# Cross-attention on one core: another order of the opening loads and query chunks, and a closing sum in two halves

## The chip, the cores and the metric

The kernel runs on one core of a Trainium2 chip. The metric is device microseconds from launch to end, the median of several runs. One execution was also taken by the hardware profiler; its trace times every instruction on the tensor engine (PE, with its weight loads shown as PEld), the vector engine (DVE), the scalar engine (ACT), GpSimd (POOL) and the sync engine (SP), and every DMA. DMAs are issued here by SP and by ACT, each through a queue of its own (q1 is SP's in the trace, q10 is ACT's).

## The reference, cut to what matters

Two token sets of 2048 rows attend with 20 heads of 32 channels to 77 text tokens and, separately, to 77 image tokens. The two attentions are added, projected by Wo, and bias and input are added.

```python
q = _split_heads(hidden_states @ Wq.T, H)                 # (2, 20, 2048, 32)
k, v = heads(text @ Wk.T), heads(text @ Wv.T)             # 77 text tokens
k_ip, v_ip = heads(ip @ Wk_ip.T), heads(ip @ Wv_ip.T)     # 77 image tokens
out = merge(attend(q, k, v)) + merge(attend(q, k_ip, v_ip))
return out @ Wo.T + bo + residual
```

## The kernel before, in words

All operands are float32 and lie with the contracted dimension first. The 640 channels are five chunks of 128 (`NC`), so one chunk holds four heads; the tokens of a batch are four blocks of 512 (`TB`). A step `u` is one channel chunk over half of a batch's tokens, that is two blocks `h` = 0, 1; there are 20 steps. Chunk number `q` is `u // 2`.

For a block and a chunk, `queries` (L193 to L205) makes five matmuls of 128x512, one for each slice of 128 input channels (`k`), into one of eight PSUM banks, and `take_queries` (L207) lets ACT copy the bank, scaled, to a tile `qT`. `project_kv` (L136) makes eight matmuls of 128x154 for the keys or values of one chunk, from the context (`wo_ct`) and a weight (in slots of `aT`). `scores` (L220) makes a group of scores: for each of up to three token tiles four matmuls, one into each bank of a half (banks 0 to 3 or 4 to 7). A group then goes through ACT, DVE and POOL for the softmax; `attend` multiplies by the values; the last stage multiplies by Wo in a scheme of sums and products (`F` words) and adds each product into its sums on DVE (`Y` words, `add_part`, L784), and a finished sum is stored by a DMA.

The order on every engine is written by hand: the opening is plain code (L522 to L558), and everything behind it is a table of words, `SCHEDULE`, that `emit` turns into instructions one after the other. `R0.0@0` is score group 0 of step 0 in banks 0 to 3, `q.1.0@0` the query chunk of step 1, block 0 in bank 0, `cq.1.0` ACT's copy of it, `K0.0` ACT's copies of the scores, `v.0.0@1` a value projection, `LK`, `LQ`, `LX` loads. Each engine runs its instructions in that order, and a semaphore wait holds up all that stands behind it on the same engine. Each hardware DMA takes the next of eight completion counters, in turn over both queues, and waits until the DMA that used that counter before has landed; so no more than eight are under way.

The opening, before: x's block 0 (`x_82` below) comes in five slices of 256 KB and the first chunk of Wq in five of 64 KB, alternating between SP and ACT (L524 to L526); then SP alone loads block 1 (`x_83`), the second chunk of Wq, the context and the two key weights in turn, then blocks 2 and 3 and the value weights. PE makes seven matmuls on zeros (L547), then three query chunks one after the other (step 0 on blocks 0 and 1, step 2 on block 0; L549 to L551), then the two key projections (L552 to L555), and the table begins with the score groups `R0.0`, `R1.0`.

## Time and profile before

| | us |
|---|---|
| three runs | 498.40, 498.75, 499.44 (median 498.75) |
| the profiled execution | 497.84 |
| its span, first to last instruction | 496.0 |
| PE busy | 489.1 (99% of the span) |
| DVE busy | 413.0 (83%) |
| POOL busy | 370.3 (75%) |
| ACT busy | 301.4 (61%) |

The profiled execution took 497.84 us, 1.84 us more than its span and 0.91 us less than the median of the runs. In the trace one float32 matmul is two records, so a query chunk is ten. A row of the timeline gives start, length, engine, line, operation, result and operands, the number of records, and in brackets how long the engine had been idle and what ended that.

### The profile page before, as it was taken

To read this page: it belongs to the slowest core of one execution; us is meant where nothing else is said; L and a number is where in the kernel's file an instruction comes from. 1 tells how busy PE (TensorE), PEld (TensorE's weight loads), DVE (VectorE), ACT (ScalarE), POOL (GpSimd) and SP (SyncE) were. 2 spreads that over 40 slices of the span, in tenths; PEclk is the share of its full clock that TensorE was granted. 3 is DMA by queue.
4 is the path that set the end of the run, shared out by engine and by line. 5 is a ranking of instruction groups with operands and counts; after the bars stand their busy time and mean duration, and the time that the engine had idled before them with its cause. 6 is when DMAs were issued, how large, how long until landed. Compare 5 with 4: busy or idle time off the path is not lost.

```text
span 496.0 us, 10378 instructions
## 1 busy us (share of the span) xinstructions
PE 489.1 (99%) x4114; PEld 288.5 (58%) x4114; DVE 413.0 (83%) x417; ACT 301.4 (61%) x929; POOL 370.3 (75%) x158
## 2 busy tenths in 40 slices
PE   8999999999999999999999999999999999999997
PEld 4676657467467556456556654754755675444442
DVE  0069999979999989979979796777999888999885
ACT  1175858977687778677999869677666962100000
POOL 0069998889988989788977798365989989249820
PEclk9999999999999999999999999999999999999999
DMA  8994404142425435395671359344551221510125
GB/s 267 351 260 128 120 3 130 49 112 74 109 65 170 125 120 165 119 380 204 194 236 49 113 159 316 133 127 140 166 174 45 62 91 42 171 63 23 43 85 211
DMA packets 67472, 69.38 MB, mean 140 GB/s; under 512 B 5472, under 2 KB 47200, under 8 KB 67424
## 3 DMA queue, kind: packets, MB, share of 16 engines
q1 hardware_dynamic: 66704, 68.00, 43.6%
q8 instruction: 32, 0.52, 0.5%
q10 hardware_dynamic: 720, 0.72, 0.5%
q14 instruction: 16, 0.13, 0.1%
HBM read 54.94 MB, written 10.49 MB: 132 GB/s over the span
## 4 chain that ended last, share of the span: by engine, by line
PE 95%; DMA 3%; SPq 1%; ACTq 0%; ACT 0%; DVE 0%; issue 0%
PE bank L199 33%; PE bank L846 11%; PE bank L330 11%; PE bank L231 11%; PE bank L488 10%; PE bank L140 9%; PE bank L469 7%; PE bank L498 3%; DMA aT<-in_L_xattn_Wk_ip_dram 2%; DMA x<-in_x_dram 1%; SPq L532 1%; ACTq L526 0%; SPq L130 0%; DVE acc L792 0%; ACT pb L243 0%
## 5 line engine op out<-in xcount | busy, mean ns | idle before, releaser
L314 POOL TENSOR_TENSOR pb<-pb,rden 128x1848 f32<-128x1848 f32 (+1 forms) x60 | 175.9, 2943 | 25.6 <-DVE rden L309 25.0
L199 PE MATMUL bank<-x,wq 128*128 128x512 f32 x400 | 179.6, 598 | 1.5 <-DMA x<-in_x_dram 1.4
L293 POOL TENSOR_TENSOR pb<-pb,mx 128x1848 f32<-128x1848 f32 (+1 forms) x42 | 128.2, 3066 | 58.5 <-DVE mx L279 58.3
L199 PEld LDWEIGHTS bank<-x,wq 128*128 128x128 f32 x400 | 73.5, 190 | 87.4 <-issue 81.6
L321 DVE STREAM_TRANSPOSE pb<-pb 128x1920 f32<-128x1920 f32 (+1 forms) x60 | 115.5, 1935 | 6.7 <-POOL pb L314 6.7
L279 DVE TENSOR_REDUCE mx<-pb 128x24 f32<-128x1848 f32 (+1 forms) x51 | 93.8, 1850 | 32.0 <-ACT pb L243 31.8
L243 ACT COPY pb<-bank 128x462 f32<-128x462 f32 (+1 forms) x204 | 87.1, 537 | 34.6 <-PE bank L231 34.0
L304 DVE TENSOR_REDUCE den<-pb 128x24 f32<-128x1848 f32 (+1 forms) x49 | 91.5, 1875 | 18.6 <-ACT pb L299 15.8
L299 ACT ACTIVATE pb<-pb 128x1848 f32<-128x1848 f32 (+1 forms) x42 | 69.3, 1651 | 18.6 <-POOL pb L293 18.5
L231 PEld LDWEIGHTS bank<-kT,qT 32*128 32x128 f32 x1280 | 45.5, 184 | 26.3 <-issue 16.6
L267 ACT ACTIVATE pb<-bank,mx 128x77 f32<-128x77 f32 x184 | 53.1, 380 | 10.8 <-DVE mx L282 10.8
L231 PE MATMUL bank<-kT,qT 32*128 32x154 f32 x1280 | 56.6, 306 | 0.3 <-ACT kT L557 0.3
L330 PE MATMUL bank<-pb,v 32*32 32x512 f32 x1600 | 55.2, 597 | 0.0
L267 ACT ACTIVATE pb<-pb,mx 128x77 f32<-128x77 f32 x160 | 47.3, 373 | 0.0
L140 PE MATMUL bank<-wo_ct,aT 128*128 128x154 f32 x320 | 45.8, 297 | 0.4 <-DMA aT<-in_L_xattn_Wk_ip_dram 0.4
L140 PEld LDWEIGHTS bank<-wo_ct,aT 128*128 128x128 f32 x320 | 42.8, 188 | 3.4 <-issue 2.2
L330 PEld LDWEIGHTS bank<-pb,v 32*32 32x32 f32 x1600 | 30.6, 103 | 21.6 <-issue 9.2
L209 ACT ACTIVATE qT<-bank 128x512 f32<-128x512 f32 x40 | 24.2, 614 | 27.4 <-PE bank L199 27.4
L267 ACT ACTIVATION_READ_ACCUMULATOR pb<-bank,mx 128x1 f32 x144 | 36.7, 258 | 0.0
L469 PE MATMUL bank<-aT,wo_ct 128*128 128x512 f32 x80 | 36.4, 595 | 0.0
L488 PE MATMUL bank<-aT,wo_ct 128*128 128x256 f32 x128 | 32.0, 384 | 0.0
L488 PEld LDWEIGHTS bank<-aT,wo_ct 128*128 128x128 f32 x128 | 23.8, 190 | 7.7 <-issue 4.5
(76 smaller groups left out, 427.9 us busy)
## 6 DMA issues: line engine op xcount, KB each, us to landing
x<-in_x_dram SPq DMA_DIRECT2D x20, 1280.0 KB, 7.3
out_dram<-acc SPq DMA_DIRECT2D x20, 256.0 KB, 2.6
x<-in_x_dram SPq DMA_DIRECT2D x18, 256.0 KB, 5.4
acc<-in_x_dram SPq DMA_DIRECT2D x16, 256.0 KB, 3.4
out_dram<-x SPq DMA_DIRECT2D x15, 256.0 KB, 2.0
v<-vS SPq DMA_DIRECT2D x160, 20.0 KB, 2.1
wq<-in_L_xattn_Wq_dram SPq DMA_DIRECT2D x9, 320.0 KB, 4.7
aT<-in_L_xattn_Wk_dram SPq DMA_DIRECT2D x5, 512.0 KB, 5.5
```

The costliest lines, as they stand in the source:

```text
L140: nc.tensor.matmul(keys_in(out), loaded[n][:, k, :], cT[:, k, :, t, :], start=(k == 0), stop=(k == NCC - 1))
L199: nc.tensor.matmul(pq, wqs[q % 3][:, k, :], xs[place_of(u, h)][:, k, :], start=(k == 0), stop=(k == NC - 1),)
L231: nc.tensor.matmul(ps[g][:, ts(t, 2 * L)], qTs[(u, h)][g * D : (g + 1) * D, ts(st, P)], kT[g * D : (g + 1) * D, c, b].rearrange("p t l -> ...
L243: nc.scalar.copy(keys_of(u, s)[:, :, g], ps[g][:, : n * 2 * L].rearrange("p (n l) -> p n l", n=n))
L267: nc.scalar.activation(row, row if ps is None else rows_in(ps[g], n)[:, t, x], AF.Exp, bias=maxs[(u, s)][:, *one], accum_out=None if den i ...
L279: nc.vector.tensor_reduce(mx, rows_of(u, s), AX.X, ALU.max, negate=negate)
L293: nc.gpsimd.tensor_tensor(rows_of(u, s), rows_of(u, s), maxs[(u, s)].unsqueeze(3).to_broadcast([P, n, 2, L]), ALU.subtract)
L304: nc.vector.tensor_reduce(den_of(u, s), rows_of(u, s), AX.X, ALU.add)
L314: nc.gpsimd.tensor_tensor(rows_of(u, s), rows_of(u, s), rdens[(u, s)].unsqueeze(3).to_broadcast([P, n, 2, L]), ALU.mult)
L321: nc.vector.transpose(p, p)
L330: nc.tensor.matmul(pa[r][g * D : (g + 1) * D, :], v4s[q % 2][rows, g, k, :], zones[rows, :, g, k, :], start=(k == 0), stop=(k == NK - 1),)
L488: nc.tensor.matmul(part, w_of[m][:, kp, op], t_of(m, b, i)[:, kp], start=(op == kp == 0 and m in (1, 2, 5)), stop=(op == 1 and kp == 1 and ...
```

## The change

In the opening the first block of x is multiplied slice by slice: for each slice of x's block 0, one matmul of step 0 and one of step 2, into two banks side by side, and the first slice in two halves of 256 tokens. The key projections follow, then the score group `R0.0`, and only then the query chunk of step 0 on block 1 (`q.0.1@4 cq.0.1`, new words in the table behind `R0.0@0`). The first three chunks of Wq lie in slots of `aT` that are free until later (`wq_first`): chunks 0 and 1 come together in rows of 1 KB, chunk 2 by itself. The context is loaded by SP and the two key weights by ACT; x's block 1, Wq's chunk 2, block 2, the value weights and block 3 follow on SP. Five matmuls on zeros stand in place of seven. Eight early `qT` tiles go to free slots of `aT` instead of the pool of five. At the end, the last product (`F32.0`) and the last sum (`Y4.0.20`) are made in two halves of 256 columns, the first half stored by SP, the second by ACT. All other words of the table stay in their order.

```diff
+    EARLY = {(2, 0): 8, (2, 1): 9, (3, 0): 10, (3, 1): 11, (4, 0): 16, (4, 1): 17, (5, 0): 18, (5, 1): 19}
+    SIDES = slice(0, HT), slice(HT, TB)
+    wq_first = aT[:, ds((NC - 2) * NHB, NHB), :].rearrange("p s t -> p (s t)")[:, : NC * 3 * P]
...
-    for k in range(NC):
-        load_x(queues[k % 2])
-        queues[1 - k % 2].dma_start(out=wqs[0][:, k, :], in_=WqT[ts(k, P), :P])
-    for _ in range(NC):
-        load_x()
-    load_wq(1)
+    for n, cols in enumerate(SIDES):
+        queues[n].dma_start(out=xs[0][:, 0, cols], in_=xT[:P, cols])
+        load_first(nc.scalar, 0, n, n + 1)
+    for k in range(1, NC):
+        load_x(queues[k % 2])
+        load_first(queues[1 - k % 2], k, 0, 2)
+    for k in (0, half):
+        load_ctx(k)
+        load_w(k // half, nc.scalar)
+    for _ in range(NC):
+        load_x()
+    nc.sync.dma_start(out=wq_first[:, :, 2], in_=WqT[:, ts(2, P)].rearrange("(k p) o -> p k o", p=P))
...
-    for _ in range(7):
+    for _ in range(5):
         nc.tensor.matmul(banks[0][:, :P], warm, warm, start=True, stop=True)
-    FIRST = ((0, 0), (0, 1), (2, 0))
-    for n, (u, h) in enumerate(FIRST):
-        queries(u, h, banks[G + n])
-        take_queries(u, h, banks[G + n])
+    first = [(2 * c, 0, banks[G + c]) for c in range(2)]
+    for n, cols in enumerate(SIDES):
+        for c, (_, _, pq) in enumerate(first):
+            nc.tensor.matmul(
+                pq[:, cols], wq_first[:, 0, c], xs[0][:, 0, cols], start=(n == 0), stop=False, skip_group_check=True
+            )
+    for k in range(1, NC):
+        for u, h, pq in first:
+            queries(u, h, pq, (k,), loose=True)
+    for u, h, pq in first:
+        take_queries(u, h, pq)
...
-        "R0.0@0 R1.0@1 K0.0 q.1.0@0
+        "R0.0@0 q.0.1@4 cq.0.1 R1.0@1 K0.0 q.1.0@0
...
+            for cols in sides:
+                nc.vector.tensor_tensor(t[:, cols], t[:, cols], ps[:, cols], op)
...
+            for queue, cols in zip(queues, sides):
+                queue.dma_start(out=outT[ts(m, P), tokens], in_=t[:, cols])
```

First place: PE in the opening, from the matmuls on zeros to the first score group. `bank_71` to `bank_74` are banks 4 to 7, `x_82` and `x_83` are x's blocks 0 and 1, and L140 (L143 after the change) is a key projection. Before:

```order
L547 MATMUL bank_67<-pb 128x128 x7
L199 MATMUL bank_71<-x_82,wq_75 128x512 x5
L199 MATMUL bank_72<-x_83,wq_75 128x512 x5
L199 MATMUL bank_73<-x_82,wq_76 128x512 x5
L140 MATMUL bank_69<-wo_ct,aT 128x154 x8
L140 MATMUL bank_74<-wo_ct,aT 128x154 x8
L231 MATMUL bank_67<-kT,qT_0_146 128x154
```

And now, up to the first matmul of the second score group, with the rows in between that only go on in the same way left out:

```order
L572 MATMUL bank_67<-pb 128x128 x5
L576 MATMUL bank_71<-x_82,aT 128x256
L576 MATMUL bank_72<-x_82,aT 128x256
...
L205 MATMUL bank_71<-x_82,aT 128x512
L205 MATMUL bank_72<-x_82,aT 128x512
...
L143 MATMUL bank_69<-wo_ct,aT 128x154 x8
L143 MATMUL bank_74<-wo_ct,aT 128x154 x8
L241 MATMUL bank_67<-kT,qT_0_152 128x154
...
L205 MATMUL bank_71<-x_83,aT 128x512 x5
L241 MATMUL bank_71<-kT,qT_0_152 128x154
```

The chunk on block 1 (`x_83`) has moved from ahead of the key projections to behind the first score group, and into bank 4 (`bank_71`), which the second score group writes next.

Second place: the issue of the DMAs in the opening, behind those of x's block 0 and Wq. Before, on SP, from the last slice of block 0 to the first ones of block 2 (`x_84`):

```order
L171 DMA x_82<-in_x_dram 128x512
L171 DMA x_83<-in_x_dram 128x512 x5
L190 DMA wq_76<-in_L_xattn_Wq_dram 128x5x128
L532 DMA wo_ct<-in_ctx_dram 128x4x308
L130 DMA aT<-in_L_xattn_Wk_dram 128x8x128
L532 DMA wo_ct<-in_ctx_dram 128x4x308
L130 DMA aT<-in_L_xattn_Wk_ip_dram 128x8x128
L171 DMA x_84<-in_x_dram 128x512 x5
```

Now on SP, with what each waits for (the counters of the DMAs eight places earlier):

```order
L174 DMA x_82<-in_x_dram 128x512 [waits DMAHW1_49]
L544 DMA wo_ct<-in_ctx_dram 128x4x308 [waits DMAHW3_49]
L544 DMA wo_ct<-in_ctx_dram 128x4x308 [waits DMAHW6_49]
L174 DMA x_83<-in_x_dram 128x512 [waits DMAHW0_49]
L174 DMA x_83<-in_x_dram 128x512 [waits DMAHW1_49]
L174 DMA x_83<-in_x_dram 128x512 [waits DMAHW2_49]
L174 DMA x_83<-in_x_dram 128x512 [waits DMAHW3_49]
L174 DMA x_83<-in_x_dram 128x512 [waits DMAHW4_49]
L560 DMA aT<-in_L_xattn_Wq_dram 128x5x128 [waits DMAHW5_49]
```

And now on ACT, ahead of its first copies:

```order
L174 DMA x_82<-in_x_dram 128x512 [waits DMAHW2_49]
L537 DMA aT<-in_L_xattn_Wq_dram 128x256 [waits DMAHW4_49]
L133 DMA aT<-in_L_xattn_Wk_dram 128x8x128 [waits DMAHW5_49]
L133 DMA aT<-in_L_xattn_Wk_ip_dram 128x8x128 [waits DMAHW7_49]
L219 ACT_TABLE_LOAD
L219 ACTIVATE qT_0_152<-bank_71 128x512 [waits PE_49]
```

The key weights (L130, L133) have moved from SP's queue to ACT's, and x's block 1 from ahead of the context to behind it; block 1's first three slices wait for DMAs that carry Wq's slice 2 and x's slices 4 and 3 of block 0, its fourth for the first half of the context.

Third place: the end. After the change PE closes with these rows (bank 2 is `bank_69`):

```order
L887 MATMUL bank_68<-pb 128x512
L887 MATMUL bank_72<-pb 128x512
L887 MATMUL bank_72<-aT,pb 128x512
L887 MATMUL bank_69<-aT,pb 128x512
L887 MATMUL bank_69<-pb,wo_ct 128x256 x2
```

And DVE with these:

```order
L830 TENSOR_TENSOR x_82<-x_82,bank_67 128x512
L830 TENSOR_TENSOR x_82<-x_82,bank_71 128x512
L830 TENSOR_TENSOR x_84<-x_84,bank_68 128x512
L830 TENSOR_TENSOR x_83<-x_83,bank_72 128x512
L830 TENSOR_TENSOR acc<-acc,bank_69 128x256 x2
```

The last matmul and the last addition were one of 128x512 each, and are now two of 128x256.

## The prediction, made before the changed kernel was run

> **What bounds the kernel now.** I read the shares of the page first, then PE's busy time in two stretches, then the timeline of the opening, and last the DMAs that the opening waits for.

> ```profile
> PE 489.1 (99%) x4114; PEld 288.5 (58%) x4114; DVE 413.0 (83%) x417; ACT 301.4 (61%) x929; POOL 370.3 (75%) x158
> 0.00:2.00 2.00, 0.95 (x4) 0.95 (x5) 0.17 (x1) 0.00 (x0) 0.83 (x6) 1.00 0.14 15
> 4.30:25.35 21.05, 18.96 (x91) 10.80 (x94) 0.00 (x0) 3.77 (x8) 0.00 (x0) 1.00 1.03 340
> 25.35:492.30 466.95, 466.86 (x4019) 274.59 (x4014) 412.12 (x415) 297.63 (x921) 369.46 (x152) 1.00 0.42 131
> ```

> The last three rows are stretches: length, busy time of PE, PEld, DVE, ACT and POOL, then granted clock, DMA share and GB/s. From 25.35 us on PE lacks 0.09 us of being busy throughout. So nothing inside the kernel can be won by taking away a wait, and whatever delays PE at 25.35 delays the end by as much, as long as the loads behind it keep up. What can change is the opening, where PE is idle for 2.09 us after its first real matmul, and the tail behind the last matmul. The opening's PE rows, with the ACT copies that PE waits for:

> ```profile
> 1.05 3.36 PE L547 MATMUL bank<-pb 128*128 128x128 f32 x14 [1.05 <-DVE pb L545]
> 4.36 2.84 PE L199 MATMUL bank<-x,wq 128*128 128x512 f32 x6
> 8.58 10.57 PE L199 MATMUL bank<-x,wq 128*128 128x512 f32 x24 [1.38 <-DMA x<-in_x_dram]
> 18.98 2.35 PE L140 MATMUL bank<-wo_ct,aT 128*128 128x154 f32 x16
> 19.18 0.60 ACT L209 ACTIVATE qT<-bank 128x512 f32<-128x512 f32 x1 [3.69 <-PE bank L199]
> ```

> ```profile
> 12.94 8.75 DMA aT<-in_L_xattn_Wk_ip_dram
> 21.69 0.04 issue
> 21.73 2.39 PE bank L140 x16
> 24.12 0.02 issue
> 24.14 0.23 ACT kT L557
> 24.37 0.04 issue
> 24.42 1.85 PE bank L231 x48
> ```

> The second fence is the chain of work that ended last: the second key weight (Wk_ip) lands at 21.69, PE projects with it for 2.39 us, waits 0.30 us for ACT's copy of the keys, and makes both first score groups in 1.85 us, 0.925 us each. The second group therefore starts at 24.42 + 0.925 = **25.35 us**, and I take that point as the mark: ahead of it stand the same three query chunks, two key projections and one score group before and after the change, behind it the same table. The opening's worth is how that mark moves.

> **The change part by part.** What stands behind Wk_ip. Before: one key projection, the copy, one score group. Now the query chunk of block 1 and ACT's copy of it too. A query chunk: 24 records from 8.58 to 18.98 are 10.40 us, 0.433 each, so ten are 4.33 us. The second score group writes bank 4, out of which `cq.0.1` copies the chunk: PE waits for a copy of 0.60 us, and 0.06 us around it (0.02 and 0.04, as around the key copy), 0.66 us. Behind that waiting matmul stands everything that PE has, and ACT's score copies `K0.0` stand behind `cq.0.1`; they end a little earlier against the mark than now, so nobody else is late. Sum behind Wk_ip: 2.39 + 0.30 + 0.925 + 4.33 + 0.66 = **8.61 us**, where it was 3.66 (25.35 − 21.69). The mark now is the landing of Wk_ip plus 8.61; the change wins at the opening only if Wk_ip lands before 25.35 − 8.61 = **16.74 us**.

> When does Wk_ip land? Before, all of it was in one queue or ahead of it. In KB: x's blocks 0 and 1 2560, two chunks of Wq 640, context 1232, two key weights 1024, together 5456 by 21.69 us, with next to nothing (15 GB/s) ahead of 2 us: 277 KB per us.

> Now block 1 is no longer ahead of Wk_ip, but beside it: block 1 is on SP, Wk_ip on ACT. What do two queues do that both have work?

> ```profile
> DMA packets 163, 0.20 MB, mean 405 GB/s; under 512 B 17, under 2 KB 80, under 8 KB 163
> q10 hardware_dynamic: 91, 0.17, 89.0%
> q1 hardware_dynamic: 72, 0.03, 22.8%
> ```

> That is 3.5 to 4.0 us, the DMA view's packets and MB by queue. The two queues had about the same number of packets, and bytes as 5 to 1, since q10 was sending rows of 2 KB and q1 of 512 B. So the engines share by packets. Wk and Wk_ip are 1024 packets of 512 B each; the context is 1024 packets (two DMAs of 512) of 1232 B, block 1 only 640 of 2 KB. By packets, the context and Wk run side by side and finish together, and then Wk_ip's 1024 packets run beside block 1's 640: block 1 is through before Wk_ip is. Its slices are issued in time, for the counters they wait on belong to the last loads of block 0 and Wq and to half the context. Wk_ip then has ahead of it or beside it 1280 + 640 + 1232 + 1024 + 1280 = 5456 KB, exactly what it had before, and lands when it did, 21.7 us. Wq's rows of 1 KB make some of it cheaper, and one slice may still fall behind (256 KB, 0.9 us); Wq's chunk 2 (320 KB) can only take part late. I take **21.5 us**, with 20.3 and 22.5 as ends. Nothing of block 1 ahead of Wk_ip is the other bound: 4176 KB, 2 + 4176/277 = 17.1 us.

> [...]

> So the mark moves to 21.5 + 8.61 = 30.11, **+4.76 us** (+3.56 to +5.76).

> Ahead of Wk_ip nothing is on the path. The two chunks on block 0 need 1920 KB, 2 + 1920/277 = 8.9 us for the last slice, and 20 records of 0.433 us: they end between 4.36 + 8.66 = 13.0 and 14.7 us (with the old 1.65 us of stalls). The first key projection waits for Wk, 4176 KB with two slices of block 1 beside it, about 17.1, and ends at 19.5, ahead of 21.5. Under that cover lie the two zero matmuls that go, and the first slice in halves (eight records of 256 columns for four of 512). The nearest rows for a 256-column record, and for a DVE operation on 256 columns against 512 (busy time in all, then mean ns of one):

> ```profile
> L488 PE MATMUL bank<-aT,wo_ct 128*128 128x256 f32 x128 | 32.0, 384 | 0.0
> L513 DVE SCALAR_TENSOR_TENSOR acc<-bank,bo_sb,acc 128x256 f32<-128x256 f32 x32 | 13.8, 473 | 6.0 <-DMA acc<-in_x_dram 3.2 <-PE bank L498 2.7
> L790 DVE SCALAR_TENSOR_TENSOR x<-x,bo_sb,bank 128x512 f32<-128x512 f32 x15 | 10.6, 739 | 0.6 <-PE bank L846 0.6
> ```

> It is at most 32.0/128 = 0.25 us against half of 0.433, so the halves cost 0 to 0.27 us, hidden; without the cover, 0.27. ACT now issues nine DMAs; at SP's 12.94 row one issue of a key weight held its queue up to 1.95 us, but ACT has nothing to copy before 13 us and needs to be done by 21. The early `qT` tiles in `aT` take away a wait that no row shows: nothing. Block 2, the value weights and block 3 land some 4 us later in bytes (4176 + 1280 + 320 + 1280 KB, 27.5 us for block 2) while PE asks for them from 31 us on: nothing.

> **The tail.** The end of the chain, and the last store in the timeline and in the DMA view (KB, us from issue to landing):

> ```profile
> 492.33 0.02 issue
> 492.35 0.69 DVE acc L792
> ```

> ```profile
> 493.07 0.33 SPq L796 DMA_DIRECT2D out_dram<-acc  x1
> ```

> ```profile
> out_dram<-acc SPq DMA_DIRECT2D x1, 256.0 KB, 2.0
> ```

> The last matmul ends at 492.33, then one addition of 0.69 us, a DMA issued at 493.07 that lands 2.0 us later, and from there 2.7 us to the program's own time of 497.84. In halves, PE ends 0 to 0.07 us later and the first half is done 0.2 us before. From 128x256 to 128x512 the other DVE form (L513 and L790 above) grows from 0.473 to 0.739, so the half addition is about 0.69 − 0.27 = 0.42 us: 0.27 won (0 to 0.34). The last DMA is half as large, on ACT; of 2.0 us, the packets of 256 KB at 390 GB/s are 0.67, so 0.2 to 0.3 won, less a slower issue on ACT (0 to 0.1). Together **−0.45 us** (−0.1 to −0.65).

> Sum: 497.84 + 4.76 − 0.45 = 502.15 for an execution like the profiled one; the median of the runs stood 0.91 above it, so **503.1 us** (501.8 to 504.4 with both ends).

> **The rivals.** (a) *Wk_ip passes block 1*, because a turn of its queue takes many packets: 17.1 to 18.7 us (the latter with a slice or two and a slow stretch), the mark +0.4 to +2.0, the median 498.7 to 500.3, near 499.5. For it: in the row at 3.5 us each DMA gave only a few packets per engine, so it does not tell a turn of one packet from a turn of a whole DMA. Against it: that row's equal counts. (b) *Faster*: the loads flow better than in the old opening. Between 22.2 and 28.4 us one queue with many DMAs ahead moved this:

> ```profile
> DMA packets 2137, 2.21 MB, mean 356 GB/s; under 512 B 116, under 2 KB 1374, under 8 KB 2137
> ```

> At 356 GB/s and with block 1 behind, 4176 KB (4.28 MB) take 12.0 us from 2 us on, so Wk_ip lands at about 14.5, and PE decides: chunks until 13.0, first projection until 15.4, the mark at 15.4 + 8.61 = 24.0, −1.35; with the tail the median is **497.0**. It decides from a landing at 16.74 on. For it: in the old opening ACT's queue ran dry after five DMAs, and now both stay full. Against it: it needs two things at once, no sharing and the best rate. (c) *PE slows down in the gaps.* The zero matmuls at the start took 3.36 us for 14 records, 0.24 each, though 128 columns at 0.433 per 512 are 0.11: an idle PE starts at half speed. The 1.38 us gap at 7.2 us did not bring that back (the 24 records behind it ran at 0.433). Now there are gaps of 2.4 to 4.1 us (13.0 or 14.7 to 17.1) and 2 us before Wk_ip; if one of them is long enough, work of 1.7 to 3.3 us behind it costs double, 504.8 to 506.4. [...] (d) *Nothing at the opening*: Wk_ip at about 16.7, so only the tail shows, 498.3.

> **How the numbers follow.** Forecast 0.50, (a) 0.20, (b) 0.15, (c) 0.09, (d) 0.06. A measurement of this kernel tells 0.2%, 1.0 us, from no change. (b) is faster, 0.15; (d) and about half of (a) are the same, 0.17; the rest is slower, 0.68. Leaving out (b) and the upper part of (c) leaves out 0.19: 498.4 to 505.5 us.

> **What would show it.** In the changed profile: Wk_ip's landing, and PE's wait in front of the second key projection, should be near 21.5 us, with an idle PE of several us between 13 and 21.5 where now there are 2.09 in all; block 1's slices should land before Wk_ip; the query chunk of block 1 should stand directly behind the first score group without a wait for its data, and 0.66 us of waiting for ACT's `qT` behind it. The last half addition should take about 0.42 us. From the mark on PE should again be dense. A landing of Wk_ip at 17 to 18 us with block 1 later would prove (a), one before 16.7 (b), records of twice 0.433 us behind a gap (c).

## The result, and the profile after

| | before | after |
|---|---|---|
| runs, median (lowest to highest), us | 498.40 (496.82 to 499.44, 7 runs) | 501.51 (501.11 to 503.24, 7 runs) |
| ratio, 95% interval | 1 | **1.0073** (1.0052 to 1.0094) |
| profiled execution / its span, us | 497.84 / 496.04 | 502.49 / 500.70 |

The change makes the kernel 0.7% slower: 3.1 us between the medians, 4.66 between the two spans. First the share of PE on the page, and PE's busy time in two stretches, cut at the mark (the start of the second score group, now 28.91 us instead of 25.35). The columns are those of the prediction's stretches.

```profile
PE 491.0 (98%) x4116; PEld 289.8 (58%) x4116; DVE 412.7 (82%) x418; ACT 301.1 (60%) x929; POOL 370.4 (74%) x158
```

```profile
3.50:28.91 25.41, 21.24 (x92) 12.36 (x91) 0.00 (x0) 3.83 (x9) 0.00 (x0) 0.93 1.03 323
28.91:497.28 468.37, 467.32 (x4016) 275.24 (x4016) 411.81 (x415) 297.25 (x921) 369.58 (x152) 1.00 0.41 129
```

Before, the stretch behind the mark took 466.95 us and PE lacked 0.09 of it; now it takes 468.37 and PE lacks 1.05. The opening has 4.17 us without PE, and a granted clock of 0.93. So three things moved: the mark by 28.91 − 25.35 = +3.56 us, the interior by about +1.40, and the tail, from the last matmul to the end of the span, from 3.72 to 3.42, −0.30. Their sum is 4.66. (25.35 is what the prediction worked out from a row of two score groups. In the trace the second group's first record starts at 25.31, which makes the three parts +3.60, +1.36 and −0.30.) The opening's PE rows:

```profile
1.05 2.50 PE L572 MATMUL bank<-pb 128*128 128x128 f32 x10 [1.05 <-DVE pb L570]
3.54 1.04 PE L576 MATMUL bank<-x,aT 128*128 128x256 f32 x2
6.53 1.84 PE L576 MATMUL bank<-x,aT 128*128 128x256 f32 x6 [1.95 <-DMA aT<-in_L_xattn_Wq_dram]
8.16 8.49 PE L205 MATMUL bank<-x,aT 128*128 128x512 f32 x16
16.49 2.27 PE L143 MATMUL bank<-wo_ct,aT 128*128 128x154 f32 x16
19.98 2.37 PE L143 MATMUL bank<-wo_ct,aT 128*128 128x154 f32 x16 [1.22 <-DMA aT<-in_L_xattn_Wk_ip_dram]
22.67 1.07 PE L241 MATMUL bank<-kT,qT 32*128 32x154 f32 x24 [0.31 <-ACT kT L589]
23.66 4.56 PE L205 MATMUL bank<-x,aT 128*128 128x512 f32 x10
28.91 1.07 PE L241 MATMUL bank<-kT,qT 32*128 32x154 f32 x24 [0.69 <-ACT qT L219]
```

PE waits for the second key weight, then everything behind it runs in a row: projection, key copy, first score group, the moved query chunk, ACT's copy of it. The chain of waits says the same with exact ends:

```profile
7.38 12.56 DMA aT<-in_L_xattn_Wk_ip_dram
19.93 0.04 issue
19.98 2.39 PE bank L143 x16
...
22.67 1.07 PE bank L241 x24
23.73 4.50 PE bank L205 x10
...
28.26 0.61 ACT qT L219
```

Wk_ip lands at 19.93 us, 12.56 after its issue; 8.98 us later the second score group starts. The DMA view from 16 to 17 us, while block 1 (SP, q1) and Wk_ip (ACT, q10) are both under way:

```profile
DMA packets 308, 0.36 MB, mean 362 GB/s; under 512 B 16, under 2 KB 170, under 8 KB 308
q1 hardware_dynamic: 154, 0.28, 80.1%
q10 hardware_dynamic: 154, 0.08, 28.3%
```

154 packets in either queue, though a packet carries 2 KB in one and 512 B in the other: in this stretch the engines shared one for one by packets, and Wk_ip got 0.08 of 0.36 MB. And the end, in the timeline:

```profile
497.32 0.75 DVE L830 TENSOR_TENSOR acc<-acc,bank 128x256 f32<-128x256 f32 x2 [1.03 <-PE bank L887]
497.76 0.33 SPq L836 DMA_DIRECT2D out_dram<-acc  x1
498.10 0.37 ACTq L836 DMA_DIRECT2D out_dram<-acc  x1
```

The first half addition starts at 497.32, only 0.04 us behind the end of the last matmul (497.28), and both together take 0.75 us where the whole one took 0.69: nothing of them lies beside PE's second half. The last store lands 1.76 us after its issue at 498.10, where the whole one took 2.01. Most of what the interior lost stands in the list of PE's waits:

```profile
PE bank L498 <- DVE acc L529: 0.7, 1, 0.7
PE bank L498 <- DVE acc L523: 0.3, 1, 0.3
```

The shorter one, at 361.98 us, is traced: the sum on DVE (L523) had waited 1.7 us for an `acc` block whose fetch landed at 360.92 us, 2.3 us behind x's block beside it (before: 0.8 us behind). The longer one, at 390.67 us, stands behind a sum (L529) that waits for no fetch: DVE reaches it at 389.85 us, 5.01 us later than before, where PE's query chunk ahead of the wait is only 4.02 us later. That DVE still carried the first delay there is likely, but not shown. None of the other profiles but one, told of below, has more than 467.4 us between mark and last matmul. I take these two waits for one execution's DMAs, not for the change.

### The profile page after: what moved, and what is told of

It is laid out like the page before. It is cut to its first block, busy times and chain, and to the rows that moved or that the text cites. A ratio compares the mean times of both kernels' runs of the same rounds, so it can differ in the third digit from the quotient of the medians.

```text
span 500.7 us, 10393 instructions
## 1 busy us (share of the span) xinstructions
PE 491.0 (98%) x4116; PEld 289.8 (58%) x4116; DVE 412.7 (82%) x418; ACT 301.1 (60%) x929; POOL 370.4 (74%) x158
## 4 chain that ended last, share of the span: by engine, by line
PE 90%; DMA 6%; DVE 2%; issue 0%; ACTq 0%; SPq 0%; ACT 0%; DVEq 0%
PE bank L205 32%; PE bank L887 11%; PE bank L241 10%; PE bank L340 10%; PE bank L498 10%; PE bank L143 8%; PE bank L479 6%; PE bank L508 3%; DMA aT<-in_L_xattn_Wk_ip_dram 3%; DMA acc<-in_x_dram 2%; DMA x<-in_x_dram 1%; DMA aT<-in_L_xattn_Wq_dram 1%; DVE mx L289 1%; DVE mx L292 0%; DVE pb L331 0%
## 5 line engine op out<-in xcount | busy, mean ns | idle before, releaser
L324 POOL TENSOR_TENSOR pb<-pb,rden 128x1848 f32<-128x1848 f32 (+1 forms) x60 | 175.9, 2943 | 25.8 <-DVE rden L319 24.1
L205 PE MATMUL bank<-x,wq 128*128 128x512 f32 x280 | 125.8, 598 | 0.1
L314 DVE TENSOR_REDUCE den<-pb 128x24 f32<-128x1848 f32 (+1 forms) x49 | 91.5, 1873 | 18.5 <-ACT pb L309 15.7
L205 PEld LDWEIGHTS bank<-x,wq 128*128 128x128 f32 x280 | 51.5, 190 | 60.3 <-issue 59.4
L309 ACT ACTIVATE pb<-pb 128x1848 f32<-128x1848 f32 (+1 forms) x42 | 69.4, 1653 | 19.6 <-POOL pb L303 19.5
L277 ACT ACTIVATE pb<-bank,mx 128x77 f32<-128x77 f32 x184 | 53.1, 382 | 11.8 <-DVE mx L292 11.8
L340 PE MATMUL bank<-pb,v 32*32 32x512 f32 x1600 | 55.2, 597 | 0.0
L205 PE MATMUL bank<-x,aT 128*128 128x512 f32 x116 | 53.4, 610 | 0.0
L241 PEld LDWEIGHTS bank<-kT,qT 32*128 32x128 f32 x1024 | 36.5, 184 | 22.6 <-issue 15.5
L143 PE MATMUL bank<-wo_ct,aT 128*128 128x154 f32 x320 | 45.7, 297 | 1.2 <-DMA aT<-in_L_xattn_Wk_ip_dram 1.2
L241 PE MATMUL bank<-kT,qT 32*128 32x154 f32 x1024 | 45.8, 307 | 1.0 <-ACT qT L219 0.7
L143 PEld LDWEIGHTS bank<-wo_ct,aT 128*128 128x128 f32 x320 | 42.8, 188 | 4.2 <-issue 2.2
L340 PEld LDWEIGHTS bank<-pb,v 32*32 32x32 f32 x1600 | 30.8, 103 | 21.5 <-issue 9.1
L205 PEld LDWEIGHTS bank<-x,aT 128*128 128x128 f32 x116 | 22.1, 196 | 24.8 <-issue 22.7
L219 ACT ACTIVATE qT<-bank 128x512 f32<-128x512 f32 x32 | 19.5, 619 | 27.3 <-PE bank L205 27.3
## 6 DMA issues: line engine op xcount, KB each, us to landing
out_dram<-acc SPq DMA_DIRECT2D x19, 256.0 KB, 2.7
x<-in_x_dram SPq DMA_DIRECT2D x17, 256.0 KB, 5.9
acc<-in_x_dram SPq DMA_DIRECT2D x16, 256.0 KB, 3.4
out_dram<-x SPq DMA_DIRECT2D x15, 256.0 KB, 2.0
```

Source lines behind the costliest of these rows:

```text
L143: nc.tensor.matmul(keys_in(out), loaded[n][:, k, :], cT[:, k, :, t, :], start=(k == 0), stop=(k == NCC - 1))
L205: nc.tensor.matmul(pq, weight_of(q)[:, k, :], xs[place_of(u, h)][:, k, :], start=(k == 0), stop=(k == NC - 1), skip_group_check=loose,)
L241: nc.tensor.matmul(ps[g][:, ts(t, 2 * L)], qTs[(u, h)][g * D : (g + 1) * D, ts(st, P)], kT[g * D : (g + 1) * D, c, b].rearrange("p t l -> ...
L277: nc.scalar.activation(row, row if ps is None else rows_in(ps[g], n)[:, t, x], AF.Exp, bias=maxs[(u, s)][:, *one], accum_out=None if den i ...
L309: nc.scalar.activation(e, e, AF.Exp)
L314: nc.vector.tensor_reduce(den_of(u, s), rows_of(u, s), AX.X, ALU.add)
```

## The experiments

The kernel before had medians of 496.8 to 497.0 us on the chips of these runs, less than in the table above, so ratios to it and the mark of each profile are compared. A mark is the start of the 25th score record; by that count it is 25.31 in the profile before. Two cautions hold throughout. The changed kernel was not run on these chips, so a ratio set against its 1.0073 takes for granted that it would stand as far above the kernel before there. And a mark belongs to one execution, in which the phase of the clock (last section) plays a part.

**Halves alone.** The closing sum and its store in two halves (`SIDES`, the `F` and `Y` edits) put onto the kernel before, the opening left as it was.

```diff
-            nc.vector.tensor_tensor(t, t, ps, op)
+            for cols in sides:
+                nc.vector.tensor_tensor(t[:, cols], t[:, cols], ps[:, cols], op)
```

> The kernel before with the closing product, sum and store in halves, and its old opening. Theory (the halves save what they saved at the end of the changed profile, where span minus last matmul went from 3.70 to 3.41 us): 0.3 us faster than before, with the last matmul at the same place and the last half addition at 0.42 us; at the limit of what can be told in the times, clear in the profile. Rival (the second queue's first DMA after a long pause costs what the halves win): the stretch behind the last matmul stays at 3.7 us.

Measured: 496.75 us, ratio 0.9994 (0.9986 to 1.0003). The tail is 3.47 us, −0.25. The opening is the old one, and shows what the old one can do:

```profile
4.38 14.38 PE L200 MATMUL bank<-x,wq 128*128 128x512 f32 x30
```

Three chunks without a gap, Wk_ip landing at 20.61 us instead of 21.69, the mark at 24.23 instead of 25.31. So the profiled execution of before, from which every rate of the prediction was taken, was itself 1.1 us late in its opening. The tail's gain is seen in the trace and is too small for the times of the runs to tell.

**Key weights on SP.** One edit on the changed kernel:

```diff
-        load_w(k // half, nc.scalar)
+        load_w(k // half)
```

> The changed kernel with one edit: both key weights are loaded by SP, in turn with the context, ahead of block 1, so nothing of block 1 runs beside them. Theory (the second key weight landed at 19.93 us because block 1's packets ran beside it on the other queue): it lands at 15.7 to 17.1 us (4176 KB from 2 us on, at 304 or 277 KB per us), PE no longer waits 1.22 us for it, and the second score group starts at 27.7 us instead of 28.91; about 1.2 us faster than the changed kernel, 1.9 us slower than before in the median (500.3). Rival (the landing is only a matter of all bytes of the opening and of the rate, and two queues feed the engines better than one): it lands at 19.5 us or later, and the time stays within 0.5 us of the changed kernel's.

Measured: 501.12 us, 1.0083 (1.0069 to 1.0097). Wk_ip landed at 16.65 us, 3.28 sooner, and PE no longer waits for keys; block 1's slices, alone now, land 0.67 us apart instead of 0.93. That the one-for-one sharing delays Wk_ip is shown. But the mark moved only to 28.68. PE's rows say why:

```profile
6.51 2.93 PE L576 MATMUL bank<-x,aT 128*128 128x256 f32 x6 [1.88 <-DMA aT<-in_L_xattn_Wq_dram]
9.23 8.68 PE L205 MATMUL bank<-x,aT 128*128 128x512 f32 x16
17.74 4.38 PE L143 MATMUL bank<-wo_ct,aT 128*128 128x154 f32 x32
```

Six half-slice records take 2.93 us, 0.49 each instead of 0.25, and the trace grants the full clock only at 12.53 (in the changed kernel's profile, behind the same five zeros, it came at 4.27): the chunks end at 17.74, and there is nothing left to gain from an early key.

**The chunk between the two projections.** The words leave the table, and the projection loop gets

```diff
+        if t == 0:
+            queries(0, 1, banks[G])
+            take_queries(0, 1, banks[G])
```

> The changed kernel's loads, but the query chunk of block 1 stands between the two key projections instead of behind the first score group. Theory (3.56 us of the loss at the opening are PE waiting: for the second key weight while the chunk, whose data is there, stands behind it, and for the copy of the chunk): the chunk runs from 18.8 to 23.3 us, the second projection to 25.7, and the second score group starts at about 27.0 us without a wait for the chunk's copy, 1.9 us earlier than 28.91; median about 499.6, 1.2 us slower than before. Rival (the loss comes from the loads alone, by the slower start of the first two chunks): the start stays above 28.4 us and the time within 0.5 us of the changed kernel's.

Measured: 499.20 us (498.82 to 501.22), 1.0054 (1.0037 to 1.0071). The profiled execution was the longest of the six, and its mark is 28.96, above the 28.4 that the rival named:

```profile
17.35 3.85 PE L143 MATMUL bank<-wo_ct,aT 128*128 128x154 f32 x16 [2.78 <-DMA aT<-in_L_xattn_Wk_dram]
21.00 4.66 PE L205 MATMUL bank<-x,aT 128*128 128x512 f32 x10
```

Wk landed at 17.22 here, where the same loads in the changed kernel's profile brought it at 15.32. A projection takes 3.85 us instead of 2.27, behind a wait of 2.78 us: half clock (0.50 from 17.98 to 21.39 us), and from here on the clock is a question of its own. When the chunk began, at 21.00, Wk_ip had been there since 20.00, so there was no wait left for it to fill. What this place is worth is therefore not shown; the lower median does not show it either, for its interval overlaps the changed kernel's.

**The chunk ahead of the score groups.**

```diff
-        "R0.0@0 q.0.1@4 cq.0.1 R1.0@1 K0.0
+        "q.0.1@4 cq.0.1 R0.0@0 R1.0@1 K0.0
```

> The changed kernel with two words of its table exchanged: the query chunk of block 1 and its copy stand ahead of the first score group, not behind it. Theory (the wait of 0.69 us for the chunk's copy and the one of 0.31 us for the keys are both lost on PE because nothing stands between): the chunk covers the copy of the keys and the first score group covers the copy of the chunk, so the second score group starts 1.0 us earlier, at 27.9 us, and the median is 1.0 us lower, 500.5. Rival (the copy is waited for wherever it stands, since the score copies stand behind it on ACT): no gain, 501.5, with a new wait of PE for ACT behind the second score group.

Measured: 500.02 us, 1.0072 (1.0056 to 1.0088).

```profile
20.11 2.38 PE L143 MATMUL bank<-wo_ct,aT 128*128 128x154 f32 x16 [1.11 <-DMA aT<-in_L_xattn_Wk_ip_dram]
22.32 4.45 PE L205 MATMUL bank<-x,aT 128*128 128x512 f32 x10
26.71 1.85 PE L241 MATMUL bank<-kT,qT 32*128 32x154 f32 x48
```

Both waits for ACT (0.31 and 0.69) are gone, since the chunk covers the key copy and the first score group covers the chunk's; the mark is 27.60, −1.3. Its ratio does not differ from the changed kernel's, so this gain rests on the trace, and on the pair that follows.

**Seven zeros, then the order too.** Onto the kernel with key weights on SP:

```diff
-    for _ in range(5):
+    for _ in range(7):
```

> The kernel with both key weights on SP (e1), with seven matmuls on zeros instead of five. Theory (with five, PE is idle from 3.4 us on and has too little to do until 12 us, so it is granted the full clock only at 12.5 us in e1, and the first chunks run at half speed): the full clock comes at about 4.3 us, as in the profiles that have it early; the two chunks end at 14.0 us instead of 17.74 (last slices at 10.5 to 11.8 us), the second projection starts when its weight lands, at 16.7, and the second score group at 25.6 us instead of 28.68: 3.1 us faster than e1, 1.0 us slower than before. Rival (the chunks of e1 are late only because their slices land late): the chunks still end at 17 us or later and the time stays within 0.5 us of e1's.

and the words in the last experiment's order on top of it:

> The same (keys on SP, seven zero matmuls), and the query chunk of block 1 with its copy ahead of the first score group. Theory (e3's gain of about 1.3 us is of another kind than e5's, so the two add): the second score group starts at 24.4 to 24.6 us without any wait behind the projections; level with before, where undisturbed openings have it at 24.2. Rival (block 1 lands too late for a chunk that early): PE waits for block 1's last slices, up to 20.1 us, and nothing is gained against e5.

Measured: 499.89 us (497.96 to 503.31 in nine runs), 1.0061 (1.0041 to 1.0081), mark 27.50; with the order 498.15, 1.0031 (1.0019 to 1.0043), mark 26.23. The order is worth 1.27 us a second time. The zeros did not bring the clock: it came at 10.28 and 10.52 us, behind gaps of 1.12 and 1.24 us in which PE waited for Wq's part of slice 0.

**One first weight.** Onto that, slice 0 of Wq for both chunks in one DMA, of rows of 1 KB:

```diff
-        load_first(nc.scalar, 0, n, n + 1)
+        if n == 0:
+            load_first(nc.scalar, 0, 0, 2)
```

> The same as e6, and Wq's slice 0 for both chunks comes in one DMA with rows of 1 KB, not in two of 512 B. Theory (the second one lands at 6.5 us, behind the first half of x's slice, and PE waits 1.6 to 2.1 us for it): PE has no wait in slice 0, starts on it at about 4 us and the chunks end 0.3 to 0.5 us sooner; the second score group starts at 24.1 us, and with the tail's 0.3 us the time is level with or up to 0.4 us below before's. Rival (the slices behind it set the pace): the chunks end when they did in e6.

Measured: 496.50 us, 0.9992 (0.9984 to 1.0001).

```profile
4.20 2.99 PE L577 MATMUL bank<-x,aT 128*128 128x256 f32 x8
7.55 7.10 PE L205 MATMUL bank<-x,aT 128*128 128x512 f32 x16 [0.36 <-DMA x<-in_x_dram]
14.49 4.65 PE L143 MATMUL bank<-wo_ct,aT 128*128 128x154 f32 x32
```

The gap shrinks to 0.36 us, the full clock comes at 6.41, the mark is 24.25: 1.98 sooner. With every fault of the new opening mended the kernel is level with before, and its mark with that of the halves alone (24.23). None of the twelve kernels of this study is shown to be faster than before.

**The same first weight, alone**, on the changed kernel:

> The changed kernel with one edit: Wq's slice 0 for both chunks comes in one DMA, as in e7; key weights on ACT, chunk behind the score group and five zero matmuls as changed. Theory (two causes lie side by side: the late second weight of slice 0 with the late full clock behind it, and the second key weight's landing at 19.9 us beside block 1; either alone sets the start of the second projection): the chunks end at 14 to 15 us instead of 16.5, and PE then only waits longer for the key weights: the second score group stays at 28.5 to 29.0 us, the time within 0.5 us of the changed kernel's, 0.7% above before. Rival (the slow start of the chunks is the whole loss): the second score group comes 1.5 to 2 us earlier.

Measured: 503.15 us, 1.0130 (1.0112 to 1.0147): *slower* than the changed kernel.

```profile
18.12 7.21 PE L143 MATMUL bank<-wo_ct,aT 128*128 128x154 f32 x32 [3.32 <-DMA x<-in_x_dram]
```

The chunks end sooner, at 14.8 us; Wk, whose packets now lie beside block 1's, lands at 17.99 (in the run with the chunk between the projections, with the changed kernel's own loads, it landed at 17.22, so not all of this delay need come from the edit); and behind the wait of 3.32 us two projections take 7.21 us instead of 4.38. Those 2.83 us are nearly all of the mark's 2.98 (31.89). The profiled execution is the second longest of the five (501.76 to 504.42). The faster start bought a longer idle wait, and the wait cost the clock (0.50 from 16.97 to 23.79 us).

**The kernel before with five zeros.**

```diff
-    for _ in range(7):
+    for _ in range(5):
```

> The kernel before with one edit: five matmuls on zeros instead of seven. Theory (those two matmuls are not padding but what brings the full clock early): PE is granted it some 3 us or more later, the records of the first chunk take twice 0.433 us for so long, and the second score group starts 0.5 to 2.5 us later than in before; slower by that. Rival (only the gap behind slice 0 in the new opening brings the half clock; dense chunks do without): no change.

Measured: 497.79 us, 1.0017 (1.0009 to 1.0026), mark 24.76, the full clock at 8.18 us. The two zeros, costed at nothing, are worth about 0.8 us by the times, when PE is dense behind them, and 0.53 us by the mark against the same opening with seven (24.23, halves alone).

**Key weights on ACT, with everything else mended**: `nc.scalar` put back into the one-first-weight kernel.

> e7, the version that is level with before, with one edit: the key weights go back to ACT's queue, beside block 1 on SP's. Theory (the two queues share the engines by packets): the first key weight lands at 15.3 to 17.2 us, the second at 19.9 to 20.1 instead of 16.72, block 1's slices 0.9 us apart instead of 0.67; the second projection waits for it, and the second score group starts at 27.5 us instead of 24.25: 3.2 us slower than e7, 0.6% slower than before. Rival (with a faster start the shared landing is early enough, or the chunk hides it): less than 1 us slower than e7.

Measured: 501.55 us, 1.0085 (1.0064 to 1.0105).

```profile
17.89 6.12 PE L143 MATMUL bank<-wo_ct,aT 128*128 128x154 f32 x32 [3.75 <-DMA x<-in_x_dram]
```

Wk lands at 17.76 instead of 13.18 and the projections start 3.40 us later: the price of the queue. They also take 6.12 us instead of 4.65: the price of the clock behind the wait (0.50 from 17.90 to 21.32 us). The next two kernels take the second away and leave the first.

**The wait filled with sixteen zero products**, added to the kernel above:

```diff
+    for _ in range(16):
+        nc.tensor.matmul(banks[3][:, :P], warm, warm, start=True, stop=True)
```

> e10 with sixteen matmuls of 128x128 on zeros between the two chunks and the first key projection, into a bank that nothing uses then: 3.5 us of work for PE in the 3.75 us that it waited for the first key weight. Theory (the wait alone costs 2.7 us less than e10 lost against e7; the rest is the half clock that the long wait brings back, 17.9 to 21.3 us in e10): the clock stays full, the first projection takes 2.3 us instead of 3.85, the second starts when its weight lands at about 20 us, and the second score group starts at 27.3 to 27.6 us instead of 29.12: 1.5 us faster than e10. Rival (the clock goes down by PE's mean load over a longer time, or the loads land later still): the first projection again takes over 3 us, and the time stays within 0.5 us of e10's.

Measured: 504.58 us, 1.0172 (1.0138 to 1.0206), all six runs at 503.8 or more. The opening did as expected, the interior did not:

```profile
14.69 3.73 PE L586 MATMUL bank<-pb 128*128 128x128 f32 x32
18.26 4.42 PE L143 MATMUL bank<-wo_ct,aT 128*128 128x154 f32 x32
```

```profile
L340 PE MATMUL bank<-pb,v 32*32 32x512 f32 x1600 | 57.3, 597 | 1.1 <-issue 1.1
```

The projections run at full speed and the mark is 27.80, −1.32. But from the mark to the last matmul it takes 470.55 us, +3.5, most of it in the 1600 small attention products (L340): 57.3 us busy where the other kernels have 55.2, and 1.1 us of idle time ended by nothing that the profile shows.

**The same wait filled with four wide ones.** Twelve instructions fewer for the same time:

```diff
-    for _ in range(16):
-        nc.tensor.matmul(banks[3][:, :P], warm, warm, start=True, stop=True)
+    for _ in range(4):
+        nc.tensor.matmul(banks[3], warm, wide, start=True, stop=True)
```

> The same fill of the same gap as with sixteen small zero products, by four of 128x512 (4 products of 0.89 us by the 0.444 us of the first chunks' rows, 3.56 us beside 3.73), so that TensorE has 12 instructions fewer ahead of the interior. The run with sixteen had the mark at 27.80 us, 1.32 us sooner than without zeros, and lost 3.5 us behind it: from the second score group to TensorE's last matmul 470.55 us where every other profile but one has 467.0 to 467.4, 1.1 us of it as two waits in the attention products (L340) for which the profile names no releaser. Theory that these stalls come from how many and where instructions stand in TensorE's stream (instructions arriving late): the mark at 27.6 to 27.9 us and 467.0 to 467.4 us behind it, a span of 498.0 to 498.5, about 1.3 us less than without zeros. Rival, that a bank or tile that the zeros hold, or a full clock from the start, brings the stalls whatever the number: 470 to 471 us behind the mark again and a span of 501 to 502. Rival, that it was one execution's chance: the times then also come out below 500.5, but the sixteen-zero kernel's six runs all lay at 503.8 or above, which speaks against it.

Measured: 499.82 us, 1.0060 (1.0043 to 1.0077), span 497.92.

```profile
14.24 3.60 PE L588 MATMUL bank<-pb 128*128 128x512 f32 x8
17.82 4.46 PE L143 MATMUL bank<-wo_ct,aT 128*128 128x154 f32 x32
```

```profile
L340 PE MATMUL bank<-pb,v 32*32 32x512 f32 x1600 | 55.2, 597 | 0.0
```

Mark 27.39, −1.73 by zeros alone, and the two medians lie 1.73 us apart (each on its own chip): the half clock behind the wait is shown, and so is its cause, the idle PE. The interior is back at 467.05 us, so the sixteen's loss hung on the number or the places of the instructions and not on the zeros. And the mark is still 3.14 us behind the kernel with key weights on SP (24.25): what the second queue costs with the clock taken out.

## Why the prediction was right, and where its sizes were off

The forecast was slower, 503.1 us with a range of 498.4 to 505.5; the kernel took 501.51. The mechanism was the one forecast. The size lies at the low end: the ends of the two terms add up to 501.7 to 504.4 (the 501.8 there is 0.1 too high), and the median is just below. Step by step:

- **The mark decides the end.** Right: +3.56 at the mark and −0.30 in the tail are 3.26 of the 4.66 us between the spans, and most of the rest is two waits (0.95 us) that no other profile repeats.
- **Two queues share by packets, so Wk_ip gains nothing from leaving SP.** Right, with 154 packets beside 154; moving the keys to SP and back (16.65 against 19.93, and 16.72 against 19.61 with the rest mended) shows it. How many packets a queue sends at a time was not shown: equal counts do not tell it. The second queue brought no bandwidth: 362 GB/s with both queues (16 to 17 us), 356 before with one (22.2 to 28.4 us).
- **Wk_ip at 21.5 us.** The term that was mis-sized: 19.93, below its own low end of 20.3. The bytes were right, the rate was not. 5456 KB by 19.93 us are 304 KB per us from 2 us on, where the prediction took 277 from the one opening that it had; the same opening in the halves-alone run gives 5456/(20.61 − 2) = 293. One profiled execution's opening was taken for its rate.
- **8.61 us behind Wk_ip.** It took 8.98. The sum leaves out the 0.04 us between the landing and the first matmul, which the 3.66 beside it contains; the copy waits were right (0.30, and 0.67 for 0.66), but a score group by itself takes 1.07 where two in a row take 1.85, so half of 1.85 was too little, and the chunk takes 4.50 for 4.33 up to the point where ACT can copy it.
- **Chunks done by 13.0 to 14.7 us, with cover behind them.** Wrong in size, and harmless here: the second Wq slice landed at 6.49, PE waited 1.95 us, fell to the half clock from 7.68 to 11.09, and ended the chunks at 16.49. Wk_ip's landing covered it. Without that cover (key weights on SP) it cost what the earlier key had won.
- **The two zeros at nothing.** True under the cover, but 0.8 us in the kernel before.
- **The early `qT` tiles and the later loads behind the mark at nothing.** Right: with the rest mended (one first weight) the stretch from the mark to the last matmul is 467.06 us, 467.01 before.
- **The tail, −0.45.** −0.30, and −0.25 with the halves alone. The step that failed is the 0.27 us for a half addition: one takes 0.42 us as worked out (in the trace 497.32 to 497.74), but in the program only the first of the two additions has a wait for PE, and it starts behind both halves of the product, so the two cost 0.06 us more than the whole. What is won is the store, 0.25 as forecast, and 0.13 us between its landing and the end of the span.
- **The 0.91 us put on top** for the median above the profiled execution had the wrong sign this time: the profiled execution after lay 0.98 above its median, no more than the interior lost by chance (1.40). Against the profiled execution's 502.49 the forecast's 502.15 is 0.34 off, but only because that chance made up for the early landing.
- **Rivals.** (a) needed Wk_ip to pass block 1: excluded by the packet counts. (b) needed block 1 behind Wk_ip: not in this kernel. (d) needed Wk_ip at about 16.7 us; it came at 19.93. (c), half clock behind a gap, was given 0.09. In the changed kernel it occurs and hides; in three of the experiments it costs 1.5 to 2.8 us. The 1.7 to 3.3 us of work that the rival lets cost double were the author's estimate and stand in no row. No one length of gap is shown for it: 1.95 us sufficed in the changed kernel and 2.78 in the chunk between, while 1.38 us in the kernel before did not; the last section reads off what seems to decide.

What stays open: why the sixteen zeros cost 3.5 us in the attention products. That PE's instructions arrive late there would fit the nameless idle time. The two waits end at 264.74 and 307.11 us, each 2.3 to 2.5 us behind the start of a 16 KB packet on queue q8, which the DMA view calls instruction (262.47 and 304.64). But the profiles before and after have 32 such packets too, and with no wait behind them two start at 263.94 and 305.54 us in the changed kernel's and two at 262.38 and 303.62 with four wide zeros, so this is only argued. The chance waits at 361.98 and 390.67 us weren't made to come again either.

## What to carry to other kernels

The load that moved to a second queue came later here, while the first queue had work for the same engines: with 154 packets of 512 B beside 154 of 2 KB, Wk_ip got 0.08 of 0.36 MB and landed at 19.93 us, where ahead of block 1 in one queue it landed at 16.65; so put what is wanted first ahead in one queue. Work that can run before a late load belongs in front of the wait for it (argued here, not shown), and if it can't, in the place where it covers another engine's copies (1.3 us in two pairs of profiles). A gap in this opening cost twice, once as idle time and once as a slower clock behind it (3.75 us idle with key weights on ACT, then a clock of 0.50, which cost 1.73 us of the mark), so an opening is to be made dense before it is made early.

## What the runs showed of the hardware

```profile
4.27:7.68 3.41, 1.46 (x7) 1.05 (x6) 0.00 (x0) 0.00 (x0) 0.00 (x0) 1.00 1.02 344
7.68:11.09 3.41, 3.41 (x6) 1.70 (x6) 0.00 (x0) 1.28 (x1) 0.00 (x0) 0.50 1.10 356
17.92:21.33 3.41, 2.19 (x17) 1.96 (x16) 0.00 (x0) 0.35 (x2) 0.00 (x0) 1.00 0.87 249
21.33:24.74 3.41, 3.10 (x35) 2.22 (x34) 0.00 (x0) 0.35 (x2) 0.00 (x0) 1.00 0.93 316
```

1.46 us busy, and the next step runs at 0.50; 2.19 us busy, and the next one stays at 1.00. The kernel with the chunk between the projections:

```profile
4.33:7.74 3.41, 1.78 (x8) 1.44 (x8) 0.00 (x0) 0.00 (x0) 0.00 (x0) 1.00 0.99 314
7.74:11.15 3.41, 3.41 (x9) 1.50 (x8) 0.00 (x0) 1.28 (x1) 0.00 (x0) 1.00 1.06 359
14.57:17.98 3.41, 0.63 (x6) 0.66 (x6) 0.00 (x0) 0.60 (x1) 0.00 (x0) 1.00 1.08 360
17.98:21.39 3.41, 3.41 (x15) 3.35 (x14) 0.00 (x0) 0.15 (x2) 0.00 (x0) 0.50 0.92 265
```

1.78 us kept the clock, 0.63 lost it. The kernel with the first weight alone shows the way back:

```profile
16.97:20.38 3.41, 2.26 (x9) 2.29 (x10) 0.00 (x0) 0.00 (x0) 0.00 (x0) 0.50 1.00 277
20.38:23.79 3.41, 3.41 (x15) 3.41 (x15) 0.00 (x0) 0.35 (x2) 0.00 (x0) 0.50 0.80 278
23.79:27.20 3.41, 3.10 (x38) 2.46 (x37) 0.00 (x0) 0.35 (x2) 0.00 (x0) 1.00 0.90 277
```

2.26 us busy did not bring the full clock back, 3.41 did. The tails bear the rule out and narrow it. In the changed kernel's last two steps PE ends with 1.49 us of work and is then idle to the end of the span:

```profile
495.79:499.20 3.41, 1.49 (x6) 0.76 (x4) 1.25 (x3) 0.00 (x0) 0.00 (x0) 1.00 0.84 304
499.20:500.70 1.50, 0.00 (x0) 0.00 (x0) 0.00 (x0) 0.00 (x0) 0.00 (x0) 1.00 0.14 46
```

So 1.49 us kept the clock, and it was still full 3.42 us behind the last matmul; with the first weight alone, 0.75 us of work in the last step lost it 2.66 us behind the last matmul (the mean clock of that profile is 0.992, where the 6.82 us at 0.50 by themselves would leave 0.993); in the kernel before, a step without work (492.41 to 495.82) lost it too. In the steps of seven profiles (these four, key weights on SP, the kernel before with five zeros, and key weights on ACT with the rest mended) the full clock was lost behind 0 to 1.46 us of work and kept behind 1.49 or more, and it was granted behind 3.20 us or more and not behind 2.26 to 2.69. (For this the raster is continued back ahead of the first change; there the clock column reads 1.00 although the records run at half speed: six half-slice records took 0.49 us each with key weights on SP.) So it is not a gap's length alone that decides: 1.95 us lost the clock in the changed kernel, where it fell with sparse work into one step. That also makes the zero products at the start a matter of luck: with seven of them, 3.36 us, the full clock came between 4.2 and 10.5 us, and soon only where the raster happened to begin with them (steps from 0.84 and 0.90 us on gave it at 4.25 with key weights on ACT and at 4.31 in the kernel before) or where the work behind them had no gap (6.41 with one first weight; 10.52 behind a gap of 1.24). The rule is read off these profiles, not tested by an experiment of its own.
